# A hybrid block on one core: how the scan stage turns its rows, and when expert weights are loaded

## The chip, the cores and the metric

The kernel runs on one core of a Trainium2 chip. The metric is the device time of one execution in microseconds; smaller is better. The engines named below are TensorE (PE, with its weight loads as PEld), VectorE (DVE), ScalarE (ACT), GpSimd (POOL) and SyncE (SP), which issues most of the DMA transfers. All arithmetic is float32.

## The reference

The input is x of 8 batches x 512 tokens x 256 features. Four residual layers follow one another: a scan layer, a mixture of experts, an attention layer, and the same mixture again.

```python
x = L0_attn_a_x
x = x + _L0_attn_a_ref(_layernorm(x), Win, bin_, Bp, Cp, Dp, Wout, bout)   # scan over tokens
x = x + _L0_ffn_ref(_layernorm(x), router_w, bias, gate_w, up_w, down_w, sh_gate_w, sh_up_w, sh_down_w)
x = x + _L0_attn_b_ref(_layernorm(x), Wqkv, Wout)                          # 16 heads, causal
x = x + _L0_ffn_ref(_layernorm(x), router_w, bias, gate_w, up_w, down_w, sh_gate_w, sh_up_w, sh_down_w)
return x
```

The scan layer projects the normalised rows to 512 channels, applies silu, runs a decaying sum over the tokens, and projects back to 256. A mixture picks 4 of 16 experts for each token by the router's scores, and adds two shared experts that every token passes.

## The kernel before

**Stages.** The kernel has four: the scan stage (`stretch(Scan())`), the first routed stage (`routed(0, ...)`, the chosen experts over sorted blocks of 128 rows), the attention stage (`stretch(Attention())`) and the second routed stage. A stretch works through the batches in one software pipeline. In iteration b of the scan stretch these run beside each other: the main work of batch b (scan), the routing of batch b - 1 (norm, scores, choices), the sends of older batches' rows to their experts (`xg`, by GpSimd's indirect DMA), the shared experts of batches further back, and the norm and turn of batch b + 1.

**The order.** `beside` mixes pieces by the number of TensorE columns that each has issued. `timed` places the steps of a piece at given shares of the iteration, so `turns = (0.75, 0.79)` means that the two steps of a turn are issued when 75% and 79% of the iteration's columns are out. A scheduler then orders the instructions of each engine. An engine runs its instructions strictly in that order, and SP issues its DMAs in that order too: an instruction that waits holds up all behind it.

**The turn.** A batch's normalised rows `xn` have tokens on the partitions. The next projection wants features there (`xT`). Two helpers do this:
- `turned` (L418): eight TensorE transposes (L430, tile pt_l) into two PSUM banks, and one ScalarE copy from each (L432).
- `by_shares` (L435): the rows are written to DRAM (L440) and read back by four DMAs (L443), one for each group of 32 partitions, so that afterwards 32x32 blocks are all that is left to turn. VectorE does that in two instructions (L452). Its two yields part the DMA issues from the VectorE work.

In before, the scan stretch uses `turned` for every batch, and the attention stretch uses `by_shares` from batch 2 on (L1435).

**Consumers of a turn.** Scan's `main` (L555): for each of four channel groups c, TensorE projects (L563, tile pz_s), ScalarE applies silu (L572, xi_s), VectorE runs the scan (L574, state_s) and combines (L578, y_s). At the end TensorE projects back (L510, py_s) and VectorE adds to x (L519).

**Other lines that the prediction names.** The router's logits are L669 on TensorE (pl_m) and L680 on VectorE (logit_m); its choices end in sel_m (L739) and a prefix sum on TensorE (L747, pr_m). The shared experts are L1146 (pg_m), L1165 (act_m), L1174 (pd_m), and their sum is stored by L1184. L487 (rstd_l) is the last VectorE step of a norm ahead of the scaling (L493). L213 is a list of constants. L1444 stores x (part<-x).

**Weights.** `w_all` holds all 16 experts. Experts 0 to 13 are loaded in the scan stretch in slots, one for each iteration (`later[b - 1 :: shares]`), directly behind the load of the batch after next (L149). The region of experts 14 and 15 first serves as a place for the turned rows of batches 0 to 5 (`kept_rows`), which the shared experts read; their loads (L235 to L237) are issued by `done_with` (L538) once the shared experts of batch 5 have been issued, and each waits for the rows it overwrites to be read. The routed stage reads `w_all` by an index known only at run time.

Of the kernel before, what the change touches and what calls it, by code (L numbers as in the profile page):

```python
# [18 lines left out]
B, T, D = 8, 512, 256  # L19
# [9 lines left out]
E, F = 16, 256  # L29
# [33 lines left out]
OUT, STAY = 2, 3  # L63
# [19 lines left out]
def tile_hybrid_block(  # L83
# [22 lines left out]
    nc = tc.nc  # L106
# [8 lines left out]
    def bank(shape, name: str, kind: str = "one"):  # L115
        kind = instead.get(kind, kind)
        return stage[kind].tile(shape, FP, tag=kind, name=name)
# [15 lines left out]
    parts = [[dram.tile([NTOK + BLK, D], FP, name=f"part_{i}_{j}") for j in range(2)] for i in range(2)]  # L133
# [6 lines left out]
    def load_x(b: int):  # L140
        x_sb = xpool.tile([P, NT, D], FP, tag="x", name=f"x_{b}")
        x_tiles[b] = x_sb
        src = x_in[b].rearrange("(t p) d -> p t d", p=P)
        if b == 0:

            for t in range(NT):
                (nc.scalar if t % 2 else nc.sync).dma_start(out=x_sb[:, t, :], in_=src[:, t, :])
            return None
        return nc.sync.dma_start(out=x_sb, in_=src)  # L149

    def rows_of(part, b: int):
        return part[b * T : (b + 1) * T, :].rearrange("(t p) d -> p t d", p=P)
# [79 lines left out]
    def load_expert(e: int):  # L232
        at = e * WEXP
        gu = w_all[:, at : at + 2 * KD * F].rearrange("p (s k f) -> p s k f", k=KD, s=2)
        nc.sync.dma_start(out=gu[:, 0], in_=gate_w[e].rearrange("(p k) f -> p k f", p=P))  # L235
        nc.sync.dma_start(out=gu[:, 1], in_=up_w[e].rearrange("(p k) f -> p k f", p=P))
        nc.sync.dma_start(  # L237
            out=w_all[:, at + 2 * KD * F : at + WEXP].rearrange("p (k d) -> p k d", k=KF),
            in_=down_w[e].rearrange("(k p) d -> p k d", p=P),
        )  # L240
# [104 lines left out]
    later = [lambda e=e: load_expert(e) for e in range(E - OUT)]  # L345
# [6 lines left out]
    shares = B - 2  # L352
# [60 lines left out]
        for _ in range(many):  # L413
            nc.tensor.matmul(idle, lhsT=ones, rhs=ones, start=True, stop=True)

    wide = []

    def turned(src, tag: str, into, copies, home=None, past=None):  # L418

# [12 lines left out]
            copies[k](dst[:, k, :], flat)  # L432
            yield T // 2

    def by_shares(src, tag: str, into, into_rows: bool, home=None):  # L435


        rows = src()
        through = dram.tile([T, D], FP, name=f"through_{tag}")
        nc.sync.dma_start(out=through.rearrange("(t p) d -> p t d", p=P), in_=rows)  # L440
        share = rows.rearrange("p t d -> p (t d)") if into_rows else kb4(f"share_{tag}").rearrange("p t d -> p (t d)")
        for a in range(QUAD):
            nc.sync.dma_start(  # L443
                out=share[a * SQ : (a + 1) * SQ, :].rearrange("s (g c) -> s g c", g=T // SQ),
                in_=through[:, a * KD * SQ : (a + 1) * KD * SQ].rearrange("(g s) c -> s g c", s=SQ),
            )
        yield 0
        dst = home() if home else work.tile([P, KD, T], FP, tag="kb4", name=f"xT_{tag}", bufs=KB)
        into(dst)
        for half in range(2):  # L450
            g = slice(half * T // SQ // 2, (half + 1) * T // SQ // 2)
            nc.vector.transpose(  # L452
                dst.rearrange("p k (g s) -> p k g s", s=SQ)[:, :, g],
                share.rearrange("p (g i k) -> p k g i", i=SQ, k=KD)[:, :, g],
            )
        yield 0

    by_both = (nc.scalar.copy, nc.vector.tensor_copy)
    by_scalar = (nc.scalar.copy, nc.scalar.copy)
# [39 lines left out]
    def kb4(name: str):  # L499
        return work.tile([P, NT, D], FP, tag="kb4", name=name, bufs=KB)  # L500
# [19 lines left out]


    class Scan:
        mixture, ahead, copies, turns = 0, 1, by_scalar, (0.75, 0.79)
        quota = (10, 10, 20)
        over, sent, begun_last = 4, 0, 4
        early = 0


# [2 lines left out]

        def load(self, b: int):
            if b + 1 < B and b > 0:
                with tc.issue_after(load_x(b + 1).ins):
                    for load in later[b - 1 :: shares]:
                        load()

        def done_with(self, b: int):  # L538
            if b == B - 3:
                for e in range(E - OUT, E):  # L540
                    load_expert(e)

        def end(self):
            pass
# [389 lines left out]
    def routed(i: int, table, beside):  # L934
# [152 lines left out]
        def run(first: int, last: int):  # L1087
# [6 lines left out]
            def load_to(n: int):  # L1094
                for m in coming:
                    load(m)
                    if m >= n:
                        break
# [32 lines left out]
    def shared_experts(i: int, b: int, xnT_of, tanh: bool):  # L1131

        tag = f"m{i}_{b}"

        def steps():
            xnT = xnT_of()
            acts = []
            for n in range(NSH):
                _, g_sb, u_sb, _ = shared[n]
                act = work.tile([P, KF, T], FP, tag="kb4", name=f"act_{tag}_{n}", bufs=KB)  # L1140
                acts.append(act)
                for f in range(KF):
                    pair = [bank([P, T], f"pg_{tag}_{n}_{f}_{which}") for which in range(2)]
                    for dst, w in zip(pair, (g_sb, u_sb)):
                        for k in range(KD):
                            made = nc.tensor.matmul(  # L1146
                                dst,
                                lhsT=w[:, k, f * P : (f + 1) * P],
                                rhs=xnT[:, k, :],
                                start=(k == 0),  # L1150
                                stop=(k == KD - 1),
                            )
                        wide[:] = [made]
                        if dst is pair[0]:
                            yield KD * T
                    ph, pu = pair
                    sig = work.tile([P, T], FP, tag="col", name=f"sig_{tag}_{n}_{f}", bufs=COLS)
                    if tanh:

                        nc.scalar.activation(sig, ph, AF.Tanh, scale=0.5)  # L1160
                        nc.vector.scalar_tensor_tensor(sig, sig, 1.0, ph, ALU.add, ALU.mult)
                        nc.vector.scalar_tensor_tensor(act[:, f, :], sig, 0.5, pu, ALU.mult, ALU.mult)
                    else:
                        nc.scalar.activation(sig, ph, AF.Silu)
                        nc.vector.tensor_mul(act[:, f, :], pu, sig)  # L1165
                    yield KD * T
            y_sb = kb4(f"ys_{tag}")
            for half in range(2):
                py = bank([P, 2, D], f"pd_{tag}_{half}")
                for j in range(2):  # L1170
                    t = 2 * half + j
                    for n in range(NSH):
                        for f in range(KF):
                            nc.tensor.matmul(  # L1174
                                py[:, j, :],
                                lhsT=acts[n][:, f, t * P : (t + 1) * P],
                                rhs=shared[n][3][:, f, :],
                                start=(n == 0 and f == 0),
                                stop=(n == NSH - 1 and f == KF - 1),
                            )  # L1180
                    yield NSH * KF * D
                nc.scalar.copy(y_sb[:, 2 * half : 2 * half + 2, :], py)

            (nc.gpsimd if b == B - 1 else nc.sync).dma_start(out=rows_of(parts[i][1], b), in_=y_sb)  # L1184

        return Piece(NSH * KF * (2 * KD * T + NT * D), steps())


# [11 lines left out]
    class Attention:  # L1200
        mixture, ahead, copies, turns = 1, 2, by_both, (0.65, 0.85)
        quota = (10, 8, 20)
        over, sent, begun_last = 0, 4, 8
        early = 2
        norms, scores, choose = (0.0, 0.12, 0.2, 0.28), (0.29, 0.45, 0.55, 0.6), (0.66, 0.95)
        last_rows, last_scores = (0.2, 0.28), (0.35, 0.38)
        bursts, parts = {}, {}

        done_with = Scan.done_with

        def end(self):
            for e in range(first_expert, E - OUT):
# [208 lines left out]
    def stretch(layer):  # L1421


        i = layer.mixture
        xT, xn, made, routes, sends = {}, {}, {}, {}, []
# [6 lines left out]
            return normed(b, f"l{i}_{b}", place, False, first)  # L1432

        def turn(b: int, copies=layer.copies):
            if i == 1 and b >= layer.ahead:  # L1435
                return by_shares(lambda: xn.pop(b), f"l{i}_{b}", lambda xnT: xT.update({b: xnT}), True)
            return turned(lambda: xn.pop(b), f"l{i}_{b}", lambda xnT: xT.update({b: xnT}), copies)

        def project(b: int):
# [63 lines left out]
        for b in range(1 if begun else 0, B):  # L1503
# [3 lines left out]
            scores, choose, turns = layer.scores, layer.choose, layer.turns  # L1507
            if i == 0 and b == 1:

                scores, choose, turns = (0.95, 0.955, 0.97, 0.975), (0.98, 0.99), (0.96, 0.965)  # L1510
# [16 lines left out]
            if b > 0:  # L1527
# [3 lines left out]
                else:  # L1531
                    first, then, rows, full = layer.norms
# [155 lines left out]
```

## Time and profile before

| | us |
|---|---|
| median of 3 runs (lowest, highest) | 1635.16 (1631.83, 1639.35) |
| the profiled execution, and its span | 1635.8, 1634.1 |
| scan stage: until the first expert matmul (ph, L1033) | 0 to 344.20 |
| first routed stage, about | 344 to 724 |
| attention stage, about | 724 to 1240 |
| second routed stage, about | 1240 to 1634 |
| TensorE busy | 1576.0 (96%) |
| VectorE busy | 1003.9 (61%) |
| ScalarE busy | 779.1 (48%) |
| GpSimd busy | 776.1 (47%) |

The span is cut into stages by the tiles that TensorE works on. A row of a timeline has a start, a length and a number of instructions; in brackets stands the idle time of the engine ahead of the row and what ended it. One fp32 matmul of the code appears as two records; a transpose appears as one. The end of a matmul record is modelled, so the distance from one start to the next is the better measure of what TensorE spends. The granted clock is 0.987 over the whole span, with 1 for full speed.

### The profile page before, as it was taken

What the parts mean: (1) busy time and instruction counts of PE and PEld (TensorE: products, weight loads), DVE (VectorE), ACT (ScalarE), POOL (GpSimd) and SP (SyncE); (2) the same over time, 40 slices, a digit from 0 to 9 for tenths busy, and PEclk for the clock granted to TensorE, in tenths of its full rate; (3) what the DMA queues carried; (4) which work ended last, traced back from release to release, by engine and by line L of the source; (5) the groups of instructions that cost most, each with busy time, mean ns of one, the idle gap of its engine ahead of it and who ended that gap; (6) DMA issues with size and microseconds to landing.
All of it is one profiled execution on the core that took longest, in us unless ns stands there. A gap on an engine that the chain in (4) does not pass through costs nothing. (4 is left out here: it accounts for less than half of the span.)

```text
span 1634.1 us, 34092 instructions
## 1 busy us (share of the span) xinstructions
PE 1576.0 (96%) x10030; PEld 1160.7 (71%) x10030; DVE 1003.9 (61%) x3264; ACT 779.1 (48%) x1622; POOL 776.1 (47%) x639
## 2 busy tenths in 40 slices
PE   8899998999999999999899999999999999999996
PEld 5466665679999999983444454544557999999995
DVE  6877764434466544437888888887844444454553
ACT  3343442235555555546544554453214555555553
POOL 4376754635556555550014432433532555555554
PEclk9999999999999999999999999999999999999998
DMA  5354433547777766641323433332744767777776
GB/s 170 125 186 154 151 103 125 181 92 108 119 117 113 104 97 99 95 65 41 86 82 111 127 108 105 110 115 100 256 144 89 107 116 113 132 138 135 133 135 133
DMA packets 282765, 196.88 MB, mean 120 GB/s; under 512 B 168688, under 2 KB 262672, under 8 KB 282576
## 3 DMA queue, kind: packets, MB, share of 16 engines
q1 hardware_dynamic: 230016, 121.50, 29.1%
q0 software_dynamic: 51984, 72.09, 24.5%
q8 instruction: 85, 1.39, 0.4%
q10 hardware_dynamic: 576, 1.05, 0.2%
q14 instruction: 104, 0.85, 0.2%
HBM read 91.29 MB, written 103.23 MB: 119 GB/s over the span
## 5 line engine op out<-in xcount | busy, mean ns | idle before, releaser
L1073 POOL DMA_INDIRECT part<-rows x272 | 426.0, 1566 | 341.8 <-ACT rows L1072 240.0
L798 POOL DMA_INDIRECT xg<-sorted_m,slots_m x256 | 270.9, 1058 | 257.1 <-ACT slots_m L795 125.6
L1033 PEld LDWEIGHTS ph<-rows,gate 128*128 128x128 f32 x2160 | 277.6, 191 | 32.6 <-ACT rows L1016 21.2
L1033 PE MATMUL ph<-rows,gate 128*128 128x128 f32 x2160 | 291.7, 278 | 0.5 <-ACT rows L1016 0.5
L1033 PE MATMUL ph<-rows,up 128*128 128x128 f32 x2160 | 285.3, 275 | 0.0
L1063 PE MATMUL pyr<-w_all,rows 128*128 x1088 | 279.5, 380 | 1.4 <-DVE rows L1043 1.4
L1033 PEld LDWEIGHTS ph<-rows,up 128*128 128x128 f32 x2160 | 262.9, 192 | 0.0
L1006 DVE COPY up<-w_all 128x512 f32 x270 | 119.8, 444 | 226.5 <-PE ph L1033 202.2
L1006 ACT COPY gate<-w_all 128x512 f32 x270 | 166.4, 617 | 124.0 <-DVE up L1006 63.7
L1043 DVE TENSOR_TENSOR rows<-ph,rows 128x256 f32<-128x256 f32 x272 | 115.5, 425 | 155.3 <-ACT rows L1041 89.3
L1295 ACT ACTIVATE w_all<-ps_a 128x1024 f32<-128x1024 f32 x160 | 155.2, 1021 | 104.5 <-PE ps_a L1285 91.2
L1063 PEld LDWEIGHTS pyr<-w_all,rows 128*128 128x128 f32 x1088 | 186.8, 192 | 15.8 <-DVE rows L1043 1.6
L1072 ACT ACTIVATE rows<-pyr,gain 128x256 f32<-128x256 f32 x272 | 128.7, 473 | 78.6 <-PE pyr L1063 59.0
L1041 ACT ACTIVATE rows<-ph 128x256 f32<-128x256 f32 x272 | 104.3, 384 | 117.3 <-PE ph L1033 99.5
L1174 PE MATMUL pd_m<-sd_sb,act_m 128*128 128x256 f32 x512 | 120.5, 385 | 5.1 <-issue 2.9
L1285 PE MATMUL ps_a<-w_all 32*128 32x384 f32 (+3 forms) x1024 | 107.5, 473 | 12.3 <-ACT w_all L1295 10.7
L1174 PEld LDWEIGHTS pd_m<-sd_sb,act_m 128*128 128x128 f32 x512 | 96.6, 192 | 29.7 <-issue 12.3
L1305 DVE SCALAR_TENSOR_TENSOR w_all<-w_all,causal 128x512 f32<-128x512 f32 (+1 forms) x160 | 92.0, 575 | 26.8 <-ACT w_all L1295 24.6
L1285 PEld LDWEIGHTS ps_a<-w_all 32*128 32x128 f32 x1024 | 46.6, 188 | 69.2 <-ACT w_all L1295 36.7
L1146 PE MATMUL pg_m<-w_all,sg_sb 128*128 128x512 f32 x192 | 92.8, 605 | 0.0
L1146 PE MATMUL pg_m<-w_all,su_sb 128*128 128x512 f32 x192 | 91.6, 599 | 0.0
L1321 PE MATMUL po_a<-w_all,v_a 128*32 128x512 f32 (+3 forms) x1024 | 91.1, 453 | 0.0
(222 smaller groups left out, 1923.2 us busy)
## 6 DMA issues: line engine op xcount, KB each, us to landing
rows<-xg SPq DMA_DIRECT2D x720, 32.0 KB
rows<-xg SPq DMA_DIRECT2D x92, 134.0 KB
part<-x SPq DMA_DIRECT2D x16, 512.0 KB
w_all<-in_L_ffn_gate_w_dram SPq DMA_DIRECT2D x29, 256.0 KB
w_all<-in_L_ffn_up_w_dram SPq DMA_DIRECT2D x29, 256.0 KB
w_all<-in_L_ffn_down_w_dram SPq DMA_DIRECT2D x29, 256.0 KB
part<-ys_m SPq DMA_DIRECT2D x14, 512.0 KB
sum<-part SPq DMA_DIRECT2D x14, 512.0 KB
```

Of the source, the lines that this page charges most:

```text
L798: nc.gpsimd.indirect_dma_start(out=xg[i], out_offset=bass.IndirectOffsetOnAxis(ap=slots[:, at : at + 1], axis=0), in_=rows[:, t, :], in_of ...
L1006: copy(here, w_all[:, bass.ds(held[n][0] + half * KD * F, KD * F)])
L1033: nc.tensor.matmul(ph[s][:, f * P : (f + 1) * P], lhsT=both[s][:, k * F + f * P : k * F + (f + 1) * P], rhs=rows[:, ROW + k * P : ROW + (k ...
L1041: nc.scalar.activation(act, ph[0], AF.Silu)
L1043: made = nc.vector.tensor_mul(act, ph[1], act)
L1063: nc.tensor.matmul(py, lhsT=act[:, f * P : (f + 1) * P], rhs=w_all[:, bass.ds(w + 2 * KD * F + f * D, D)], start=(f == 0), stop=(f == KF - 1),
L1072: nc.scalar.mul(y, py, gain[:, TK : TK + 1])
L1073: acc = nc.gpsimd.indirect_dma_start(out=parts[i][n % 2], out_offset=bass.IndirectOffsetOnAxis(ap=rows[:, D + 2 * TK : D + 2 * TK + 1].bit ...
L1146: made = nc.tensor.matmul(dst, lhsT=w[:, k, f * P : (f + 1) * P], rhs=xnT[:, k, :], start=(k == 0), stop=(k == KD - 1),)
L1174: nc.tensor.matmul(py[:, j, :], lhsT=acts[n][:, f, t * P : (t + 1) * P], rhs=shared[n][3][:, f, :], start=(n == 0 and f == 0), stop=(n == ...
L1285: nc.tensor.matmul(ps[j // 2][:, j % 2, col : col + n], lhsT=k_sb[w][r, o, c * P : (c + 1) * P], rhs=q_sb[r, o, c * P : T], start=True, st ...
L1295: nc.scalar.activation(es[two], ps[two], AF.Exp, scale=ATT_SCALE)
```

## The change

From batch 3 on (`through = 3`), the scan stretch turns its rows with `by_shares` instead of `turned`. The two steps of a turn are placed at 0.66 and 0.92 of the iteration instead of 0.75 and 0.79; this holds for batch 3 and later, since batch 2's turn has places of its own. `by_shares` gets a hook, `then`, which is called with the last share's load. In the iterations in which it turns batches 3 to 6, the slot's expert weights are issued behind that load, and no longer behind the load of x. The loads of experts 14 and 15 are issued behind the store of batch 5's shared sum. The attention stretch takes the same rule with `through = 2`, which gives what it did before, and its hook does nothing.

```diff
-    def by_shares(src, tag: str, into, into_rows: bool, home=None):
+    def by_shares(src, tag: str, into, into_rows: bool, home=None, then=lambda load: None):
...
         for a in range(QUAD):
-            nc.sync.dma_start(
+            load = nc.sync.dma_start(
                 out=share[a * SQ : (a + 1) * SQ, :].rearrange("s (g c) -> s g c", g=T // SQ),
                 in_=through[:, a * KD * SQ : (a + 1) * KD * SQ].rearrange("(g s) c -> s g c", s=SQ),
             )
+        then(load)
         yield 0
...
     class Scan:
-        mixture, ahead, copies, turns = 0, 1, by_scalar, (0.75, 0.79)
+        mixture, ahead, copies, turns = 0, 1, by_scalar, (0.66, 0.92)
...
+        through = 3
...
         def load(self, b: int):
             if b + 1 < B and b > 0:
-                with tc.issue_after(load_x(b + 1).ins):
+                x_load = load_x(b + 1)
+                if b < self.through:
+                    self.load_more(b, x_load)
+            if b == B - 1:
+                return
+
+        def done_with(self, b: int):
+            if b == B - 3:
+                with tc.issue_after(stored[-1].ins):
+                    for e in range(E - OUT, E):
+                        load_expert(e)
+
+        def load_more(self, b: int, past):
+            if 0 < b < B - 1:
+                with tc.issue_after(past.ins):
                     for load in later[b - 1 :: shares]:
                         load()
-
-        def done_with(self, b: int):
-            if b == B - 3:
-                for e in range(E - OUT, E):
-                    load_expert(e)
...
-            (nc.gpsimd if b == B - 1 else nc.sync).dma_start(out=rows_of(parts[i][1], b), in_=y_sb)
+            stored[:] = [(nc.gpsimd if b == B - 1 else nc.sync).dma_start(out=rows_of(parts[i][1], b), in_=y_sb)]
...
         def turn(b: int, copies=layer.copies):
-            if i == 1 and b >= layer.ahead:
-                return by_shares(lambda: xn.pop(b), f"l{i}_{b}", lambda xnT: xT.update({b: xnT}), True)
+            if b >= layer.through:
+                return by_shares(lambda: xn.pop(b), f"l{i}_{b}", lambda xnT: xT.update({b: xnT}), True, then=lambda load: layer.load_more(b, load))
             return turned(lambda: xn.pop(b), f"l{i}_{b}", lambda xnT: xT.update({b: xnT}), copies)
```

In the order of instructions on each engine this gives: on TensorE the 40 transposes of batches 3 to 7 are gone, and the rest up to the routed stage stands as before; on ScalarE their ten copies are gone; on VectorE two transposes (L453 in the changed kernel) stand ahead of the first state_s of batches 3, 4, 5, 6 and 7; on SP one write and four share loads for each of these batches stand ahead of the slot's weights, and the six loads of experts 14 and 15 stand together behind the store of batch 5's shared sum, ahead of the 16 zero fills of `xg` (L846).

More of the change, by code (lines that the diff above doesn't have):

```diff
@@ L414, in keep_busy @@
             nc.tensor.matmul(idle, lhsT=ones, rhs=ones, start=True, stop=True)
-    wide = []
+    wide, stored = [], []
     def turned(src, tag: str, into, copies, home=None, past=None):
@@ L1203, in tile_hybrid_block @@
         over, sent, begun_last = 0, 4, 8
+        through = 2
         early = 2
@@ L1209, in tile_hybrid_block, with load_more @@
         done_with = Scan.done_with
+        def load_more(self, b: int, past):
+            pass
         def end(self):
```

## Prediction

> **What bounds the kernel now.** I read the busy table, then the busy time by stretch (one scan batch each), then the two timelines around the point where a batch's rows are turned. TensorE is busy 1576 of 1634.1 us. The change lies in the scan stage, the first 340 us, so that stage is read alone. In the stretches by batch the columns are TensorE, its weight loads, VectorE, ScalarE and GpSimd busy us (count), granted clock, DMA share, GB/s:
>
> ```profile
> 127.58:161.68 34.10, 34.10 (x141) 22.35 (x140) 24.50 (x85) 14.56 (x36) 24.05 (x24) 1.00 0.49 165
> 161.68:195.77 34.09, 34.09 (x141) 22.40 (x140) 25.56 (x88) 14.65 (x36) 23.43 (x24) 1.00 0.50 167
> ```
>
> TensorE has no gap in a whole batch, so its instructions are the length of the batch. VectorE, at 25 of 34 us, looks to have room, but what matters is where in the batch that room lies. TensorE's timeline before batch 5's first projection (pz_s; start, us, line, operation, tiles):
>
> ```profile
> 152.12 1.88 PE L1146 MATMUL pg_m<-w_all,su_sb 128*128 128x512 f32 x4
> 153.84 1.12 PE L430 MATMUL pt_l<-ident,xn 128*128 128x128 f32 x8
> 154.79 1.89 PE L510 MATMUL py_s<-w_scan,y_s 128*128 128x256 f32 x8
> 156.52 1.88 PE L1146 MATMUL pg_m<-w_all,sg_sb 128*128 128x512 f32 x4
> ...
> 161.68 1.88 PE L563 MATMUL pz_s<-xT_l,w_scan 128*128 128x512 f32 x4
> ```
>
> The eight transposes hold TensorE from 153.84 to 154.79, 0.95 us, and end 6.9 us ahead of the projection that needs them. VectorE in the same place:
>
> ```profile
> 151.31 0.32 DVE L680 STREAM_TRANSPOSE logit_m<-pl_m 128x128 f32<-128x128 f32 x1 [3.83 <-PE pl_m L669]
> 152.80 0.69 DVE L519 TENSOR_TENSOR x<-py_s,x 128x512 f32<-128x512 f32 x1 [1.18 <-PE py_s L510]
> ...
> 163.51 0.69 DVE L1165 TENSOR_TENSOR act_m<-pg_m,sig_m 128x512 f32<-128x512 f32 x1
> 164.12 0.16 DVE L487 TENSOR_SCALAR rstd_l<-mv_l 128x4 f32<-128x4 f32 x1
> 164.32 1.22 DVE L574 TENSOR_TENSOR_SCAN state_s<-decay,xi_s 128x512 f32<-128x512 f32 x1
> ```
>
> From 152.80 to 165 VectorE has no gap: its room lies before 151.31, where it waited 3.83 us for the router's logits. It leaves rstd_l at 164.25, 2.6 us **after** TensorE has begun the projection. That is harmless now, since the projection waits for ScalarE's copies (done at 155.7).
>
> **Part 1: batches 3 to 7 turned by VectorE.** Removed: 5 x 8 transposes. The row says 0.95 us per eight, 118 ns each, so 4.7 us of TensorE time that has nothing beside it. [...] ScalarE loses 10 copies x 0.587 = 5.9 us. It is busy 14.6 of 34 us and no TensorE gap here ends on it: nothing.
>
> Added: two VectorE transposes per batch, and in the order of instructions of the changed kernel they stand **directly ahead of state_s of the next batch**, behind act_m and rstd_l. The first of TensorE's projections now waits for both. The attention stage already does this, with the same shapes (L452), so their price is known:
>
> ```profile
> 778.09 1.30 DVE L452 STREAM_TRANSPOSE xT_l<-xn 128x512 f32<-128x512 f32 x2
> 801.97 1.30 DVE L452 STREAM_TRANSPOSE w_all<-share_m 128x512 f32<-128x512 f32 x2 [1.25 <-DMA share_m<-through_m]
> ```
>
> A pair takes 1.30 us; to it I add 0.1 for the hand-over (VectorE's sel_m ends at 262.34, TensorE's pr_m starts at 262.39). For batch 5: VectorE free at 164.2, pair done 165.5, projection at 165.6. TensorE, without its transposes, is ready at 161.68 - 0.95 = 160.73. It stands idle for 4.9 us, and the batch ends 165.6 - 161.68 = 3.9 us later than before. Nothing moves VectorE forward: its dense run starts on TensorE's py_s, and from there it has 11.4 us of work plus the pair, TensorE 8.6 us (160.73 - 152.12).
>
> The other batches by the same two timelines (VectorE free / projection before / projection then / lost):
> - batch 3: 97.9 / 92.15 / 99.3 / 7.1. VectorE works off a list of constants (L213) ahead of the pair, and it stood idle for 2.83 us before L519 at 94.42 although py_s had ended at 90.6. If that wait goes, 4.3; I take 5.7.
> - batch 4: 129.4 / 127.58 / 130.8 / 3.2, without the 1.01 us that act_m waited there.
> - batch 6: 197.9 / 195.77 / 199.3 / 3.5.
> - batch 7: its L519 waits for TensorE, so VectorE comes 0.95 earlier: 231.4 / 231.43 / 232.8 / 1.4.
>
> Sum 5.7 + 3.2 + 3.9 + 3.5 + 1.4 = 17.7 us lost, the 4.7 us gain already in it. Behind the waiting projection stand pg/pd and py_s of the same batch, behind the transposes state_s; both want that projection anyway, so the delay is counted once. From the projection on to the next logits the distances stay (state_s starts 2.6 us after the projection in both), except that batch 3's late state_s no longer makes TensorE wait 0.52 us at 112.8: -0.5.
>
> **The clock.** The gaps would be 6.6, 4.2, 4.9, 4.5 and 2.4 us. The trace has two such stalls in the scan. One of 2.66 us, followed by transposes, ends in the first stretch; the other, of 4.56 us, comes ahead of the second (TensorE busy, granted clock, DMA share, GB/s):
>
> ```profile
> 76.00:81.00 5.00, 4.62 (x25) 0.66 0.49 162
> 262.00:268.60 6.60, 6.21 (x17) 0.50 0.13 45
> ```
>
> Lost: 0.34 x 5.0 = 1.7 us and 0.5 x 6.6 = 3.3 us, mean 2.5. [...] By the two rows it is all four long ones. I take 2.5 x 2.5 = 6 us; ends 2 x 1.7 = 3 and 4 x 3.3 = 13.
>
> **Part 2: DMA of the turned rows.** Per batch 512 KB out in rows, 512 KB back in four shares of 256-byte pieces. The one pair of the attention stage that waited for its shares came 12.1 us after the write's issue (789.87 to 801.97). Here VectorE needs them 14.9 to 20 us after xn is made (xn of batch 4 at 114.5, VectorE free at 129.4). Cost nothing. If the cover fails, VectorE stops with everything behind it, 1 us for 1 us.
>
> **Part 3: a slot's weights behind the shares.** SP issued batch 5's slot at 142.7 to 146.3, and now does so some 9 us later. The batch's part<-x follows at 162.5, the next x load at 176; nothing reads these weights before the routed stage (VectorE's first copy of w_all, 337.2). Nothing; it clears the queue for the shares.
>
> **Part 4: the last two experts' six loads.** SP issued them between 209.3 and 291.1, each waiting for kept rows to be read. Now all stand behind the store of batch 5's shared sum (300.3) and ahead of the 16 zero fills (303.5 to 319.0): 6 x 0.4 = 2.4 us on SP, and 1.5 MB at the 351 GB/s seen at 81 to 84 us is 4.5 us. SP's next time that matters is 334.67, where it waits for the block table: 15 us of cover, and 25 us before 337.2. Nothing; without cover the routed stage starts later by the excess. The stores queued behind the old waits have no reader before the routed stage.
>
> **Sum.** 17.7 - 0.5 + 6 = 23 us on the profiled execution's own 1635.8 (span 1634.1): 1659. The median of the runs is 0.6 lower; within rounding I keep **1659**. Behind the scan TensorE runs nearly without gaps to the end, so the loss is passed on.
>
> **Rivals.**
> - *Clock stays at full rate*: the same stalls without the clock term, 1653. [...] Chance 0.25, against 0.40 for the forecast.
> - *Half rate after all four long stalls*, 3.3 us each: 1635.8 + 17.2 + 13 = 1666. For: both stalls in the trace were followed by it. 0.13.
> - *Shares late*: GpSimd's scatter packets share the engines (DMA busy half the time in the scan, against gaps in attention); 2 us late in each batch is +10: 1669. 0.07.
> - *A later wait swallows part of it*: at 257.83 TensorE waits 4.56 us for sel_m, then half rate, 7.9 us together. If the shifted work meets no such wait: 1651. 0.08.
> - *The cover holds, faster*: VectorE's pair ends before TensorE gets there, only the transposes go: 1635.8 - 4.7 - 0.5 = 1631. It decides from VectorE being free 1.4 us ahead of TensorE, at 159.3 for batch 5, where it was at 164.2; it would have to lose 5 us of the 11.4. Only batch 7 comes near. 0.05.
> - *The stall eats just the gain*: VectorE is free some 4 us earlier than in the trace, so that a wait of about 1 us a batch pays for the transposes: 1636. 0.02.
>
> A measurement here tells 0.5% (8 us) from no change. Slower by more: 0.93, the first five cases. The case of 1631 is 0.3% faster and so mostly inside the bound: within 0.05, faster 0.02. The range 1644 to 1671 takes in both clock ends, batch 3's two values and the swallowed wait, and leaves out the fast side.
>
> **What would show it.** Right: no pt_l between 80 and 230 us; a gap of 4 to 5 us in TensorE ahead of pz_s of batches 4, 5 and 6, released by VectorE's L453 pair; some of them followed by clock 0.50; the first ph of the routed stage near 367 instead of 344.20. Wrong: pairs that end before TensorE is ready, an idle VectorE ahead of L453 released by the share DMAs, or gaps at the routed stage's start.

## The result, and the profile after

| | before | after |
|---|---|---|
| median, us (lowest, highest) | 1634.52 (1631.83, 1639.35), 4 runs | 1662.99 (1661.67, 1664.29), 4 runs |
| ratio to before, 95% interval | | 1.0166 (1.0150 to 1.0182) |
| profiled execution, span, us | 1635.8, 1634.1 | 1664.3, 1662.6 |
| granted clock over the span | 0.987 | 0.976 |
| start of the first expert matmul (ph) | 344.20 | 370.58 |

The change makes the kernel 28 us slower, and 26.4 us of that are there when the scan stage ends. The later stages keep their lengths: 379.8 and 380.0 us (first routed stage), 515.8 and 516.4 us (attention), 394.2 and 395.0 us (second routed stage).

The same two stretches of the kernel after, one batch each, with the columns as before (TensorE, weight loads, VectorE, ScalarE, GpSimd busy us, then granted clock, DMA share, GB/s):

```profile
136.66:175.88 39.22, 34.77 (x132) 21.92 (x133) 26.67 (x88) 13.49 (x34) 22.62 (x24) 0.94 0.52 167
175.88:216.52 40.64, 35.64 (x132) 22.24 (x133) 26.05 (x88) 13.59 (x34) 23.15 (x24) 0.92 0.52 161
```

TensorE has some nine records fewer and is yet busy for longer: a batch holds 4 to 5 us of idle time, and its clock is no longer 1. TensorE's timeline (start, us, line, tiles, in brackets the idle time ahead and what ended it) shows where, in the first projection of each batch from 3 to 7:

```profile
96.66 3.75 PE L574 MATMUL pz_s<-xT_l,w_scan 128*128 128x512 f32 x4 [7.37 <-DVE xT_l L453]
...
102.78 1.88 PE L574 MATMUL pz_s<-xT_l,w_scan 128*128 128x512 f32 x4
...
136.66 3.35 PE L574 MATMUL pz_s<-xT_l,w_scan 128*128 128x512 f32 x4 [4.03 <-DVE xT_l L453]
...
175.88 3.75 PE L574 MATMUL pz_s<-xT_l,w_scan 128*128 128x512 f32 x4 [4.45 <-DVE xT_l L453]
...
216.52 3.75 PE L574 MATMUL pz_s<-xT_l,w_scan 128*128 128x512 f32 x4 [5.00 <-DVE xT_l L453]
...
256.60 1.95 PE L574 MATMUL pz_s<-xT_l,w_scan 128*128 128x512 f32 x4 [2.68 <-DVE xT_l L453]
```

Each waits for VectorE's pair of turns, 23.5 us together. Behind the four gaps of 4 us and more the projection takes up to twice its time (3.35 to 3.75 in place of 1.88 us), at a granted clock of 0.50 to 0.58 over its first 3.3 us; behind the one of 2.68 us it takes 1.95 us, at 1.00. VectorE ahead of batch 5's projection:

```profile
171.64 0.68 DVE L520 TENSOR_TENSOR x<-py_s,x 128x512 f32<-128x512 f32 x1
172.24 0.57 DVE L750 TENSOR_REDUCE sel_m<-pick_m 128x64 f32<-128x256 f32 x1
172.73 0.74 DVE L469 BATCH_NORM_STATS2 stats_m<-x 128x6 f32<-128x256 f32 x2
...
173.47 0.66 DVE L1176 TENSOR_TENSOR act_m<-pg_m,sig_m 128x512 f32<-128x512 f32 x1
...
174.33 0.16 DVE L488 TENSOR_SCALAR rstd_l<-mv_l 128x4 f32<-128x4 f32 x1
174.43 1.30 DVE L453 STREAM_TRANSPOSE xT_l<-xn 128x512 f32<-128x512 f32 x2
```

VectorE has no gap here. The pair takes its 1.30 us and is simply the last of a long list. The view of who waits for whom, for line L453 in the scan stage, says the same: nothing stands under "its engine sat idle before it", and under "who waited for it" there is one line (us, times):

```profile
  PE pz_s L574: 23.5, 5
```

So the shares were there when VectorE came to them.

In batch 3 the list is not the whole of it. There VectorE stood idle for 2.18 us ahead of the pair, at its sum into x:

```profile
91.17 0.69 DVE L520 TENSOR_TENSOR x<-py_s,x 128x512 f32<-128x512 f32 x1 [2.18 <-remote]
```

"remote" is the profile's word for a releaser that it doesn't name. Waits of this kind come up again below.

### The profile page after: what moved, and what is told of

It reads as the page before. It is cut to its first block, busy times and chain, and to the rows that moved or that the text cites. A ratio compares the mean times of both kernels' runs of the same rounds, so it can differ in the third digit from the quotient of the medians.

```text
span 1662.6 us, 34060 instructions
## 1 busy us (share of the span) xinstructions
PE 1584.9 (95%) x9990; PEld 1161.0 (70%) x9990; DVE 1007.8 (61%) x3274; ACT 775.1 (47%) x1612; POOL 772.9 (46%) x639
## 5 line engine op out<-in xcount | busy, mean ns | idle before, releaser
L1320 DVE SCALAR_TENSOR_TENSOR w_all<-w_all,causal 128x512 f32<-128x512 f32 (+1 forms) x160 | 91.7, 573 | 29.4 <-ACT w_all L1310 27.3
```

## The experiments

In what follows a gap is idle time of TensorE. The theory to be tested, **T**: the loss is TensorE waiting for a pair that stands late in VectorE's order, with half clock behind the longer waits. The rivals: **R1**, the transfers of the turned rows decide; **R2**, the late loads of experts 14 and 15 cost it; **R3**, the clock has no price of its own. The runs come in groups, each with runs of the kernel before on the same chip. On the chip of the first group the kernel before takes 1616.5 us, in the other groups 1636 to 1638, so the ratio to before is what is compared.

### The last two experts' loads alone

The kernel before, with part 4 only:

```diff
-                for e in range(E - OUT, E):
-                    load_expert(e)
+                with tc.issue_after(stored[-1].ins):
+                    for e in range(E - OUT, E):
+                        load_expert(e)
...
-            (nc.gpsimd if b == B - 1 else nc.sync).dma_start(out=rows_of(parts[i][1], b), in_=y_sb)
+            stored[:] = [(nc.gpsimd if b == B - 1 else nc.sync).dma_start(out=rows_of(parts[i][1], b), in_=y_sb)]
```

> The kernel before, with only the last two experts' six loads moved behind the store of the shared sum; rows turned on TensorE as before. Theory T (the added time is TensorE waiting for VectorE's two turns ahead of the projections of batches 3 to 7): none of it is here, so the time of before, 1634 us, within 3 us. Rival R2 (late weights of experts 14 and 15 cost it): part or all of the 28 us appears here, at the start of the second experts' work or as a wait of TensorE on w_all; 1640 to 1662 us.

Measured: 1617.84 us, ratio 1.0005 (0.9995 to 1.0015). R2 falls; part 4 costs nothing.

### The turn by memory alone, with the weights at their old place

The kernel after without its parts 3 and 4:

```diff
                 x_load = load_x(b + 1)
-                if b < self.through:
-                    self.load_more(b, x_load)
-            if b == B - 1:
-                return
+                self.load_more(b, x_load)
...
-                with tc.issue_after(stored[-1].ins):
-                    for e in range(E - OUT, E):
-                        load_expert(e)
+                for e in range(E - OUT, E):
+                    load_expert(e)
...
-                return by_shares(..., True, then=lambda load: layer.load_more(b, load))
+                return by_shares(..., True)
```

> The turn by way of memory alone: the shares of batches 3 to 7 as in the kernel after, but a slot's weights are issued straight behind the load of x as in the kernel before, which puts them ahead of the shares on SyncE's queue, and the last two experts' loads are at their old place. VectorE's order is the same as in the kernel after. Theory T: the shares may land some 6 us later and still lie ready before VectorE comes to the pair, so the gaps ahead of the projections stay as they are (2.7 to 7.4 us, 22 to 25 us in all) and the time is that of the kernel after, 1661 to 1666 us. Rival R1 (the transfer decides: how early the shares are issued sets when the pair can run): the pair waits for a DMA, the gaps grow by up to 6 us each, 1675 to 1690 us.

Measured: 1641.5 us, ratio 1.0156 (1.0139 to 1.0173): the whole loss. Between the write of batch 3's rows and its first share lie 7.8 us here (79.11 to 86.88), where the kernel after had 5.3 (76.16 to 81.48), so the weights do slow the shares. What VectorE and TensorE waited for at the pair, in the scan stage:

```profile
its engine sat idle before it (us, times) until:
  DMA xn<-through_l: 0.8, 1
who waited for it (us, times):
  PE pz_s L570: 18.6, 5
```

Only one pair waited for its shares, 0.8 us, in batch 3. The gaps were 5.4, 3.2, 4.4, 3.3 and 2.2 us, 18.6 together, which is less than the 22 to 25 expected; but the ratio is that of the kernel after. Batch 3's gap is 2 us shorter than in the kernel after, and VectorE has no wait of the kind "remote" ahead of that pair here. R1 falls for the kernel as it stands, and parts 3 and 4 neither made the loss nor eased it.

### The gaps filled

The kernel after, with eleven matmuls of a constant tile ahead of the first projection:

```diff
+                if b >= self.through:
+                    keep_busy(11, f"gap_{tag}")
```

> The kernel after, with 11 products of a constant tile (128x128, 222 ns each, some 2.4 us) put on TensorE straight ahead of the first projection product of batches 3 to 7, so that of each gap at most 5 us is idle. They compute nothing that is used. Theory T with a price for the clock: the projections still start when VectorE's pair is done (the gaps plus fill stay 22 to 25 us in all), but the granted clock behind the gaps no longer falls to half, so up to the 9 us that the projections lose to half clock come back: 1653 to 1658 us. Rival R3 (no price for the clock: the stall alone is the loss, and products stretched behind a gap are stretched for another reason): the same as after, 1661 to 1666 us. If fill runs late and stands in the way: above 1666 us.

Measured: 1631.35 us, ratio 1.0089 (1.0072 to 1.0106), so 10 us below the run before on the same chip (which is without parts 3 and 4, and these made no difference to the time). TensorE's busy time around the five projections (length, busy us and count, granted clock, DMA share, GB/s), first with the gaps open (the turn by memory alone):

```profile
91.00:103.00 12.00, 9.15 (x28) 0.73 0.18 61
130.00:142.00 12.00, 9.72 (x31) 0.86 0.18 63
168.00:180.00 12.00, 8.49 (x18) 0.72 0.13 44
208.00:220.00 12.00, 9.52 (x22) 0.86 0.16 55
247.00:259.00 12.00, 9.82 (x27) 1.00 0.23 79
```

and with the gaps filled:

```profile
94.00:106.00 12.00, 10.07 (x44) 1.00 0.40 144
130.00:142.00 12.00, 11.29 (x55) 1.00 0.37 133
168.00:180.00 12.00, 10.00 (x37) 1.00 0.21 77
205.00:217.00 12.00, 11.22 (x46) 1.00 0.31 110
243.00:255.00 12.00, 12.00 (x49) 1.00 0.23 78
```

The clock column is the difference: 1.00 throughout. The projections still wait for the pair: the gaps left are 1.93, 0.71, 2.00, 0.78 and none, and with 2.4 us of fill ahead of each that is the same stall of some 17.6 us. So the clock has a price of its own, and R3 falls. The distance from the first to the second projection product gives it directly. At full clock it is 3.44 us. With the gaps open it was 5.37, 4.93, 5.78, 5.07 and 3.51 (7.5 us lost), with the gaps filled 3.43 to 3.52 (0.3 us). That is 7.2 of the 10 us; 1 us is the somewhat shorter stall; the rest is left open.

### The pair ahead of the top-8 search, with earlier norms

The kernel after, with the next batch's statistics and rows earlier, and the search held behind the pair:

```diff
-        mixture, ahead, copies, turns = 0, 1, by_scalar, (0.66, 0.92)
+        mixture, ahead, copies, turns = 0, 1, by_scalar, (0.36, 0.6)
...
-            nc.vector.transpose(
+            pairs[tag] = nc.vector.transpose(
...
-            nc.vector.max(best[:, t, :], s[:, t, :])
+            with behind_pair(i, b):   # issue_after the pair of batch b + 2
+                nc.vector.max(best[:, t, :], s[:, t, :])
...
-                    timed(norm(nxt), *spread(stats, 0.44, NT), *spread(0.56, 0.64, NT)),
+                    timed(norm(nxt), *spread(0.02, 0.08, NT), *spread(0.20, 0.28, NT)),   # from batch 3 on
```

> The kernel after, with the statistics and rows of the next batch normed earlier in a step (places 0.02 to 0.08 and 0.20 to 0.28), the turn placed at 0.36 and 0.60, and the router's top-8 search of a slot held in order behind the pair of turns. The same instructions; on VectorE the pair stands ahead of the search and of all behind it, some 5 us earlier for batches 4 to 7 than in the kernel after. Theory T: the gaps ahead of the projections of batches 4 to 7 fall from 4.0, 4.5, 5.0 and 2.7 us to 0 to 1 us each, the half clock behind them with it, batch 3 stays or gains a little: 1636 to 1646 us. Rivals R1 and R2: the gaps do not depend on where the pair stands in VectorE's order: 1660 us or more, with the pair waiting for the shares. If the router's chain, now later by a pair of turns (2.6 us), becomes the wait: gaps at sel_m's products instead, 1645 to 1660 us.

Measured: 1627.07 us, ratio 1.0065 (1.0048 to 1.0082). The gaps of batches 4 to 7 fell to 0.37, 0.82, 0 and 0 us, as T has it. Batch 3 kept 3.31 us with half clock, because there the 20 instructions of L213 still stand ahead of the pair; with a few others among them they take 2.9 us (88.55 to 91.50). And a new wait came: the transposes of batch 2's rows for the router (pt_m) waited 3.1 us in three pieces, 2.16 the longest, since VectorE now scaled xn in the middle of making these rows.

### The pair somewhat earlier

The same places for norm and turn, but nothing held behind the pair.

> The kernel after with the next batch's statistics and rows placed earlier (0.02 to 0.08, 0.20 to 0.28) and the turn at 0.36 and 0.60, but nothing held in order behind the pair: on VectorE the pair then stands behind the router's search and its sel_m, ahead of the statistics that came before it, some 2 to 2.6 us earlier than in the kernel after and some 2.5 us later than in the run with the pair ahead of the search. Theory T (the gap is as long as VectorE's order makes it): a dose between the two, gaps of batches 4 to 7 each about 2 to 2.6 us shorter than in the kernel after (about 2, 2, 2.5 and 0.3 us), mostly too short for half clock; a ratio of 1.008 to 1.011. If the place on VectorE has a threshold and no dose (all or nothing): 1.0065 or 1.016.

Measured: 1671.45 us, ratio 1.0209 (1.0185 to 1.0232): slower than the kernel after, and the expectation was wrong. The gaps of batches 3 to 7:

```profile
102.58 3.75 PE L574 MATMUL pz_s<-xT_l,w_scan 128*128 128x512 f32 x4 [9.79 <-DVE cand_at L213]
...
144.07 2.52 PE L574 MATMUL pz_s<-xT_l,w_scan 128*128 128x512 f32 x4 [2.54 <-DVE xT_l L453]
...
184.49 3.75 PE L574 MATMUL pz_s<-xT_l,w_scan 128*128 128x512 f32 x4 [5.35 <-DVE xT_l L453]
...
224.06 3.53 PE L574 MATMUL pz_s<-xT_l,w_scan 128*128 128x512 f32 x4 [3.60 <-DVE xT_l L453]
...
263.22 1.95 PE L574 MATMUL pz_s<-xT_l,w_scan 128*128 128x512 f32 x4 [2.45 <-DVE xT_l L453]
```

Batch 3's wait grew to 9.79 us, and batch 5's was no shorter than before. What was earlier in VectorE's order was not earlier in time. VectorE ahead of batch 5, and GpSimd in the same place:

```profile
174.81 0.69 DVE L520 TENSOR_TENSOR x<-py_s,x 128x512 f32<-128x512 f32 x1 [4.67 <-remote]
```

```profile
171.41 0.96 POOL L809 DMA_INDIRECT xg<-sorted_m,slots_m  x1 [0.30 <-issue]
172.68 0.96 POOL L809 DMA_INDIRECT xg<-sorted_m,slots_m  x1 [0.30 <-issue]
173.66 1.04 POOL L489 TENSOR_TENSOR rstd_l<-rstd_l,neg_half 128x4 f32<-128x4 f32 x1
```

VectorE stands idle for 4.67 us at the start of its dense run, and goes on at 174.81, when GpSimd's half of the norm's rstd step (L489) has ended at 174.70. That step stood behind a series of GpSimd's sends at 1.27 us each. Batches 4 and 6 show the same (135.21 and 135.25, 215.92 and 215.98). It looks as if the earlier norm had tied VectorE to GpSimd's queue, but two things in the traces speak against it. In the run with the pair ahead of the search, which has the same early norms and the same order on VectorE at this place, VectorE goes on without a wait, 4 us before GpSimd's step ends:

```profile
158.74 0.69 DVE L524 TENSOR_TENSOR x<-py_s,x 128x512 f32<-128x512 f32 x1
```

```profile
161.70 1.11 POOL L493 TENSOR_TENSOR rstd_l<-rstd_l,neg_half 128x4 f32<-128x4 f32 x1
```

And the kernel before, with its late norms, has such a wait too, of 3.85 us, which ends at 259.82, where no step of GpSimd ends. In the scan stage (60 to 340 us) the four traces of the first group's chip show no wait of VectorE or ScalarE with this releaser, the nine other traces each show at least one (2.18 and 1.73 us ahead of batch 3's pair in the two of the kernel after). So these waits, 4.67 us and less, are part of this run's loss, but what makes them stays open. This run does not contradict T, and it doesn't measure by how much a gap shrinks for each step forward of the pair.

### The same, with memory only from batch 4 on

The run with the pair ahead of the search, with `through = 4` and batch 3's norm and turn at their old places.

> As the run with the pair ahead of the top-8 search, but batch 3 is turned on TensorE again as in the kernel before (memory from batch 4 on), since there the pair stood behind 14 instructions that make constants and its gap of 3.3 us with the half clock behind it was what remained of the loss. Theory T: no gaps of over 1 us ahead of any projection; the four batches save about 0.9 us of transposes each, less some 1 us of short gaps: a ratio of 0.997 to 1.000, 1 to 4 us below the kernel before. If the loss of that run was elsewhere (the late loads or the scan's other order): still 1.004 or more.

Measured: 1649.82 us, ratio 1.0063 (1.0044 to 1.0083); wrong again. Batch 3's projection had no gap now, but pt_m waited 2.94 and 2.16 us, batch 5's projection 2.80, and pd_m 3.04 us with half clock behind it. The row on VectorE that starts this, in the middle of batch 3:

```profile
107.96 0.41 DVE L498 TENSOR_SCALAR sorted_m<-x,mv_m,rstd_m 128x256 f32<-128x256 f32 x1 [1.77 <-DMA xg<-sorted_m,slots_m]
108.29 0.75 DVE L593 SCALAR_TENSOR_TENSOR y_s<-state_s,bc_sb,xi_s 128x512 f32<-128x512 f32 x1
108.95 1.38 DVE L498 TENSOR_SCALAR xn<-x,mv_l,rstd_l 128x256 f32<-128x256 f32 x4
```

The router's rows wait for GpSimd's send to free their tile, and then the early xn stands between them. Ahead of batches 5 and 6 VectorE also stood idle for 4.14 and 3.99 us until "remote", as in the run above. So the loss was not at batch 3 alone: the early rows of xn brought a wait of their own, and the waits without a named cause came on top.

### The kernel after once more

> The kernel after, unchanged, beside the others of this call on one chip. Its ratio to the kernel before was 1.0166 (1.015 to 1.0182); it should be there again. Its gaps ahead of the projections of batches 3 to 7 are the measure for the other runs here: 7.4, 4.0, 4.5, 5.0, 2.7 us in the first profile.

Measured: 1663.27 us, ratio 1.0152 (1.0130 to 1.0175); gaps 7.10, 5.18, 3.97, 5.21 and 2.61 us.

### Only the pair moved, to the front

The norms stay at their old places. The second step of the turn is placed right behind the first, and the search, the sum into x and the activations of the shared experts are held behind the pair:

```diff
-        mixture, ahead, copies, turns = 0, 1, by_scalar, (0.66, 0.92)
+        mixture, ahead, copies, turns = 0, 1, by_scalar, (0.66, 0.70)
...
+            with behind_pair(i, b):
+                nc.vector.max(best[:, t, :], s[:, t, :])
...
+            with behind_newest():   # issue_after the newest pair of the scan stage
+                nc.vector.tensor_add(rows, py, rows)
...
+                        with behind_newest():
+                            nc.vector.tensor_mul(act[:, f, :], pu, sig)
```

TensorE's order is the same as in the kernel after.

> The kernel after with TensorE's order and all rows and statistics at their old places, and only VectorE's order changed: the second place of the turn is 0.70, and the top-8 search, the sum of the scan's output into x and the activations that come later in the step are held behind the pair, so that for batches 3 to 7 the pair stands right behind the choice of groups, ahead of the search (and, for batch 3, of the constants). That is some 6 us earlier than in the kernel after; the shares, issued by 123.1 us for batch 4, should have landed by then. Theory T (the pair's place in VectorE's order makes the stall): gaps ahead of all five projections 0 to 1.5 us, no half clock behind them, sel_m some 1.3 us later and just in time; 0.997 to 1.003. If VectorE then waits for the shares (rival R1): gaps of 1.5 to 3 us with a DMA as what VectorE waits for, 1.004 to 1.010. If what was displaced becomes the wait (the lesson of the two runs that moved the norms): gaps at sel_m, act_m or sorted_m of over 2 us, 1.004 to 1.012.

Measured: 1629.61 us beside 1638.38 for the kernel before, ratio **0.9941 (0.9921 to 0.9962)**. TensorE around batch 5's projection, and VectorE in the same place:

```profile
151.49 1.89 PE L520 MATMUL py_s<-w_scan,y_s 128*128 128x256 f32 x8
153.22 1.88 PE L1168 MATMUL pg_m<-w_all,su_sb 128*128 128x512 f32 x4
154.94 1.88 PE L584 MATMUL pz_s<-xT_l,w_scan 128*128 128x512 f32 x4
```

```profile
150.97 0.64 DVE L737 SCALAR_TENSOR_TENSOR s_m<-sel_gm,s_m 128x64 f32<-128x64 f32 x1
152.94 1.31 DVE L460 STREAM_TRANSPOSE xT_l<-xn 128x512 f32<-128x512 f32 x2 [1.33 <-DMA xn<-through_l]
154.18 0.65 DVE L530 TENSOR_TENSOR x<-py_s,x 128x512 f32<-128x512 f32 x1
154.75 0.31 DVE L745 MAX8 best_m<-s_m 128x8 f32<-128x16 f32 x3
```

The pair ends at 154.25, 0.7 us before TensorE needs it. None of the five projections waits, and the granted clock is 1.00 from 90 to 250 us. VectorE now does wait for shares, 9.0 us in four of the five batches, and that is free because TensorE isn't there yet. So T holds: with all parts of the change in place and TensorE's order untouched, the loss is gone once the pair stands early on VectorE.

### The same from batch 4 on

`through = 4`, and batch 3 turned on TensorE.

> The same order on VectorE, with the turn by memory from batch 4 on (batch 3 on TensorE as before). Theory T: as the run beside it, with one saving of 0.95 us of transposes less and no risk at the constants of batch 3: 0.997 to 1.002. If batch 3's turn by memory is what still costs there, this one is the faster by over 2 us.

Measured: 1633.9 us, ratio 0.9968 (0.9950 to 0.9985). Not faster than the run above; batch 3's turn by memory costs nothing there.

### The pair first, with the weights ahead of the shares

Part 3 undone in the version with the pair first:

```diff
-                if b < self.through:
-                    self.load_more(b, x_load)
+                self.load_more(b, x_load)
...
-                return by_shares(..., True, then=lambda load: layer.load_more(b, load))
+                return by_shares(..., True)
```

> The kernel with the pair first on VectorE, but a slot's weights issued straight behind the load of x again, so ahead of the shares on SyncE's queue and on the DMA engines. In the run with the turn by memory alone this put 7 to 9 us between the write of a batch's rows and the first share's issue, in place of 3 to 5. With the pair late in VectorE's order that cost nothing. Theory T (two arrivals at one point, the later one counts): with the pair early, VectorE now waits for the shares of batches 3 to 6 some 3 to 6 us past the time at which TensorE is ready (batch 7 has two late weight loads only and stays), with half clock behind most of the gaps: 15 to 25 us on top of the run with the pair first, a ratio of 1.003 to 1.010. If the weights' place is worth nothing even here: 0.992 to 0.997.

Measured: 1660.89 us, ratio 1.0148 (1.0120 to 1.0175), 31 us above the run beside it and more than expected. The pair's waits in the scan stage, first with the weights behind the shares, then with the weights ahead of them:

```profile
its engine sat idle before it (us, times) until:
  DMA xn<-through_l: 9.0, 4
who waited for it (us, times):
```

```profile
its engine sat idle before it (us, times) until:
  DMA xn<-through_l: 26.4, 4
who waited for it (us, times):
  PE pz_s L583: 14.9, 4
```

VectorE's wait grows by 17.4 us, and TensorE waits 14.9 us for batches 3 to 6. Half clock behind three of these gaps costs 6.7 us more, by the distances. What the expectation left out is what else stands behind the waiting pair on VectorE: act_m, for which TensorE waits 4.53 us at 233.13 (1.31 in the run beside it), with half clock behind it, 5.4 us together. These three make 27 us. From the last product ahead of batch 3's projection to the last products ahead of sel_m, TensorE's way is 27.2 us longer than in the run beside it. Here R1 is the cause, and part 3 of the change is worth about 27 us, which it could not show as long as the pair came later than the shares. Another 6 us stand at sel_m, for which TensorE waits 4.40 us here, with half clock behind it, and 0.88 us in the run beside it. The kernels before and after have this wait too (4.56 and 4.48 us), so it is not shown to come from the weights.

### The pair first once more

> The kernel with the pair first on VectorE, unchanged, beside the other of this call. Its ratio was 0.9941 (0.9921 to 0.9962); it should be there again.

Measured: 1629.99 us beside 1636.09, ratio 0.9965 (0.9949 to 0.9982). The gain is there again, at 6 us where the first time had 9. Transposes explain at most 4.7 of it. The wait for sel_m at the end of the stage, 4.56 us in the kernel before, is 1.92 and 0.88 us in these two runs; but it is 0.89 us in the run with the late loads alone too, with the old order, on the first group's chip. In the kernel before it stands behind the wait for "remote" at 259.82. So the rest of the gain is not shown to be due to the order.

## Why the prediction was right

- **Part 1, the stall.** Right in place, cause and size. Gaps predicted 6.6, 4.2, 4.9, 4.5, 2.4 (22.6 us together), measured 7.37, 4.03, 4.45, 5.00, 2.68 (23.5), each ended by the pair. Batch 3 was a compromise: 5.7 us lost lay between 4.3 and 7.1, according to whether an idle time of VectorE ahead of the pair would go or stay. It was 6.4, with 2.18 us of idle time left; in the turn by memory alone, without idle time there, the gap is 5.43 and the loss so 4.5. For the others the method was sound: VectorE's dense run starts when TensorE hands over py_s, so the distance from there to the pair could be read in the kernel before.
- **Removed transposes.** 4.7 us by the row. That they are worth about this much shows in the version with the pair first: from batch 3's first projection to batch 7's it takes 135.92 and 135.86 us in place of 139.28, so 3.4 us less, with 3.8 us of transposes gone from this stretch.
- **The clock: right in kind, too small in size.** The prediction took 2.5 of the four long gaps at 2.5 us, 6 us in all. All four were followed by half clock, with 2.7, 1.5, 2.3 and 2.5 us lost, and 0.1 behind the short one: 9.0. No run shows the 2.5 stalls of the sum, which were the author's estimate; the runs show half clock behind each long gap of the kernel after, in both its profiles. So the number of stalls with half clock was too small, and the price of one about right (2.25 on average). The rival with half rate after all four long stalls, which had a chance of 0.13, is what happened; its price of 3.3 us was too high. The measured 1663 lies 4 us above the forecast and 3 us below this rival, so it is in part luck that the forecast came so close: it stood midway between no half clock at all (1653) and half clock behind all four (1666). By distances the sum is 23.5 + 9.0 - 4.7 - 0.5 = 27.3, and the two traces give the same for the stretch of batches 3 to 7. The whole stage grew by 26.4, since the kernel after came to batch 3 some 2.1 us sooner in its profiled execution and lost 1.1 us behind batch 7. Of the 5.5 us between the predicted 23 and the measured 28.5 the clock is 3.0 and the stalls 1.1. The run with filled gaps shows the price as one of its own.
- **Part 2, the shares.** Right that they are hidden, and why: they had landed before VectorE came to them. The clause "if the cover fails, VectorE stops with everything behind it" is what the run with the weights ahead of the shares shows: there the pairs waited 26.4 us for their shares, and act_m behind them made TensorE wait 4.53 us in place of 1.31.
- **Part 3, no cost.** Right for this kernel. It is also no gain there, and a large one once the pair comes early.
- **Part 4, no cost.** Right: 1.0005 on its own. In the kernel after the six loads were issued at 325.4 to 329.0 and the zero fills from 331.1; SyncE's next wait was at 361.1.
- **The swallowed wait.** It was not swallowed in this pair of executions: TensorE waited 4.48 us for sel_m in the kernel after, 4.56 before. On the first group's chip this wait was 0.88 us with the turn by memory alone, and 0.89 us with the late loads alone.
- **"Nothing moves VectorE forward."** True for the order the scheduler chose, not for the work itself. The rival in which the cover holds needed VectorE 5 us earlier at batch 5; putting the pair ahead of the search, the sum into x and act_m gave that, and the gain was there twice (0.9941 and 0.9965), though only the transposes' part of it is accounted for. The scheduler had put the pair last although its data lay ready.

## What to carry to other kernels

When a step moves from the engine that sets the length to one with room, its share of busy time says little: read where the room lies, from the event that starts the receiving engine's dense run to the place of the new instruction in its order, and compare that with the time at which the bounding engine needs the result. A short instruction that many wait for belongs at the front of that run, and what can wait is to be held behind it by name; moving whole pieces of work earlier only moved the wait (here to pt_m, 3.1 us). A consumer starts at the later of two arrivals, so a change that brings one forward (here the shares, ahead of the weights) can measure as nothing until the other comes forward too, and is then worth a lot, here about 27 us.

## What the hardware showed beyond that

The half clock behind a gap was less a matter of chance than the prediction's 2.5 of four long gaps made it. Over eight profiled runs (the kernel after twice, the turn by memory alone, the filled gaps, the two with earlier norms and the search held, the one with earlier norms alone, and the pair first with the weights ahead), all 19 gaps of 3.2 to 9.8 us ahead of a projection were followed by a first pair of products 1.5 to 3.0 us longer than the 3.44 us at full clock. Of 15 gaps of 0.4 to 2.8 us one was, of 2.54 us (5.21 us for the two products). No gap between 2.8 and 3.2 us came up ahead of a projection. It is not so at every place: half clock also followed 1.64 us ahead of the transposes pt_m at 308.08 in the kernel after (granted clock 0.53 and 0.61 in the two stretches of 2 us from 310 to 314), and 1.99 us ahead of pd_m at 218.99 in the run with the pair ahead of the search (0.61 and 0.54 from 219 to 223; the ten records of the row took 4.11 us, where behind a gap of 1.33 us in the kernel after ten took 2.43). What sets these apart from the short gaps that passed has not been tested.
